# Layer 1 attention: the weights of each unit's last chunk are summed by TensorE instead of GpSimd

## The chip, the core and the metric

The kernel runs as one program on one core of a Trainium2 chip. Its engines are TensorE (PE, with PEld for its weight loads), VectorE (DVE), ScalarE (ACT), GpSimd (POOL) and SyncE (SP), which issues the transfers; each has its own queue and runs it in order, and they meet at semaphores. The metric is the time of one execution on the device in microseconds, the median of several. A profiled execution has a time of its own, and the lines shown come from one such execution.

## The reference

Two layers of attention over a picture of 2 batches, 256 channels and 64 x 64 places (4096 positions). The first layer has four heads of 16, a layer norm, a gate and a sigmoid; the change does not touch it. The second layer is

```python
qkv = einsum('oc,bchw->bohw', w_qkv, x) + b_qkv
q, k, v = split(qkv.reshape(b, 4, 3 * 64, 4096), 3, axis=2)
attn = softmax(einsum('bhdn,bhdm->bhnm', q, k) / 8, axis=-1)
out = einsum('bhnm,bhdm->bhnd', attn, v).reshape(b, 256, 64, 64)
return einsum('oc,bchw->bohw', w_out, out) + b_out + x
```

The softmax divides by the sum over all 4096 keys of the exponentials. It is these sums whose making is changed. All values are 32-bit floats.

## The kernel before, in words

**Units, chunks, steps.** Layer 1 works through 32 units: a batch, a pair of heads, and one of eight blocks of 512 queries. A unit goes over its 4096 keys in 32 chunks of 128, numbered 0 to 31. A chunk is a tile of 128 keys x (2 heads x 512 queries). Two chunks make a step, so a unit has 16 steps. The order of all work is written out by hand: the loop over steps at the end of the layer (L1219) calls the functions for the two chunks, here named first and second, at fixed places, and `at(step, place, ...)` hangs other work into the places "start", "early", "early end", "late" and "late end". Every engine keeps this order.

**What a step does.** `score` (L850) makes the scores of both chunks on PE into a tile of PSUM each; there are two such tiles, so the next scores wait until ACT has copied these out. `keep` (L867): DVE takes the running maximum (L878) over the chunk, then ACT copies the scores (L879) into a ring of 24 tiles called raw. Ten steps later, when the maximum over half of the chunks (16) is known, `shift` (L942) lets DVE subtract it in place (L944), `weigh` (L951) lets ACT take the exponential in place (L956), and `gather` (L970) lets PE multiply the weights with the values (av, L978). The maximum of a half reaches DVE through `turn_max`, `fold`, `split`, `turn` and `spread_shift`: PE turns it, DVE and POOL finish it, and a last product (L939) spreads it over the partitions. For the first half of a unit that product stands in step 10 of the unit itself. So a unit is weighed ten to eleven steps behind its scores, and its last two chunks (30 and 31) are gathered in step 10 of the next unit.

**The sums.** In `weigh`, after the exponential, POOL adds the chunk into an accumulator of its half (L966 for the first two chunks of a half, L968 for the others), so 30 adds a unit. In step 12 of the next unit `total` (L998) lets PE sum each accumulator over its 128 partitions by a product with ones (L1008, four products) into a tile called sum1, which `keep_total` (L1013) lets ACT copy out. The result then is turned and inverted, and scales the rows of the output (L1049). Near the end of the last unit, from chunk number `LATE` on, some chunks are not added by POOL: `on_tensor` (L948) picks them, and `gather` lets PE sum them directly by products of the weights with ones (L988) into a tile late_sums. Chunk 31 of the last unit is one of them.

**The bank that others share.** `misc` (L787) is a pool of a single PSUM tile. Keys and values of a later head pair (k1p, v1p: steps 4 to 7, in the first 24 units), queries (q1p, steps 14 and 15), the turned maxima (rt, nm1p: steps 0, 1, 8, 9), sum1 (step 12), the turned sums and outputs (steps 13 and 14) and the output projections take it in turn; the next user's first product waits until the last reader of the user before is done.

**The output projections.** The eight output blocks of batch 0 are projected while units 18 to 21 run, two in each: `fetch_output` (L1099) loads the block, `project_out` (L1081) lets PE make a half of the channels (L1083, in two products), `output` (L1089) lets DVE add bias and input (L1091) and stores the block after the second half. A block's first half is hung into step 3 or 11 of a unit, its second half into step 7 or 15.

Of the kernel before, what the change touches and what calls it, by code (L numbers as in the profile page):

```python
# [8 lines left out]
F32 = mybir.dt.float32  # L9
# [6 lines left out]
P = 128  # L16
NB = 512
# [10 lines left out]
def conv_attention_kernel(  # L28
# [20 lines left out]
    B, _, N = x.shape  # L49
    NJ = N // NB  # L50
    NM = N // P
# [75 lines left out]
    for s in range(3):  # L127
        t = const_prep.tile([P, CC, P], F32, tag=f"wpad{s}", name=f"wpad{s}")
# [27 lines left out]
    for i in range(2):  # L156
        t = const0.tile([P, PB, P], F32, tag=f"negmax0_{i}", name=f"negmax0_{i}")
# [66 lines left out]
    def at(t, place, step):  # L224
        extras.setdefault((t, place), []).append(step)
# [19 lines left out]
    with own0:  # L245
# [322 lines left out]
        for n, u in enumerate(units0):  # L568
# [6 lines left out]
            if u == units0[-1]:  # L575
                t1 = t0 + NM + 9
# [5 lines left out]
            else:  # L582
                t1 = t0 + NM + 15
# [79 lines left out]
        def misc(name):  # L663
            return small_bank[0](name)

        def fetch(key, src, tag="xb", bufs=3, pool=l1x):
            t = pool.tile([P, CC, NB], F32, tag=tag, bufs=bufs, name=f"{tag}_{key}")
            nc.sync.dma_start(out=t, in_=src.rearrange("(c p) n -> p c n", p=P))
            loaded[key] = t
# [52 lines left out]
        for i in range(NJ):  # L722
            k = (0, 0, i)
            t1 = T0 + 2 + 2 * i
# [3 lines left out]
            t1 = T0 + 20 + 3 * i if i < PB else END0 + (2, 3, 4, 9)[i - PB]  # L728
# [45 lines left out]
    END = len(units) * US  # L774


    LATE = len(units) * NM - 2 * LAG
    with (
        tc.tile_pool(name="l1", bufs=2) as l1,
# [9 lines left out]
        avs1, srows, losts, joined, halves = {}, {}, {}, {}, {}  # L789
# [13 lines left out]
        first, begun = {}, set()  # L803
# [37 lines left out]
        def next_queries(u, c):  # L841
            b, g, j = u
            if c == 0:
                q = l1x.tile([P, NB], F32, tag="q", name=f"q1_{b}_{g}_{j}")
                qs1[u] = q, misc(f"q1p_{b}_{g}_{j}")
            project_in(qs1[u][1], loaded["q", u], g, 0, c)
            if c == CC - 1:
                loaded.pop(("q", u))
# [99 lines left out]
        def on_tensor(t):  # L948
            return t >= LATE and (t % 2 == 1 or t < LATE + 4)

        def weigh(t):  # L951
            u = b, g, j = units[t // NM]
            m = t % NM
            n = m // GS
            p = raws[t]
            seq(nc.scalar.activation(p, p, AF.Exp, scale=D1**-0.5))  # L956

            if on_tensor(t):
                return
            if (u, n) not in first:  # L960
                first[u, n] = p
            elif (u, n) not in accs:
                accs[u, n] = l1.tile(
                    [P, 2, NB], F32, tag="acc", bufs=3, name=f"acc_{b}_{g}_{j}_{n}"
                )
                seq(nc.gpsimd.tensor_tensor(accs[u, n], first[u, n], p, ALU.add))  # L966
            else:
                seq(nc.gpsimd.tensor_tensor(accs[u, n], accs[u, n], p, ALU.add))  # L968

        def gather(t):  # L970
            u = b, g, j = units[t // NM]
            m = t % NM
            n = m // GS
            if m % GS == 0:
                avs1[u, n] = psv.tile([P, NB], F32, tag="av", name=f"av1_{b}_{g}_{j}_{n}")
            v = vs[b, g, m // PB]
            for k in range(2):
                seq(nc.tensor.matmul(  # L978
                    avs1[u, n][k * D1 : (k + 1) * D1, :], v[:, m % PB, k, :], raws[t][:, k, :],
                    start=(m % GS == 0), stop=(m % GS == GS - 1),  # L980
                ))
            raws.pop(t - 1, None)
            if on_tensor(t):
                if u not in srows:
                    srows[u] = psp.tile([P, 2, NB], F32, tag="pair", name="late_sums")[:, 0, :]
                for k in range(2):
                    r = D1 * n + 32 * k
                    seq(nc.tensor.matmul(  # L988
                        srows[u][r : r + 32, :], ones[:, :32], raws[t][:, k, :],
                        start=r not in begun, stop=False, skip_group_check=True,  # L990
                    ))
                    begun.add(r)
            if m % GS == GS - 1:
                a = l1.tile([P, NB], F32, tag="avs", name=f"avs1_{b}_{g}_{j}_{n}")
                seq(nc.scalar.copy(a, avs1.pop((u, n))))
                avs1[u, n] = a

        def total(u):  # L998


            b, g, j = u
            late = u in srows
            if not late:
                srows[u] = misc(f"sum1_{b}_{g}_{j}")
            for n in range(NG):
                for k in range(2):
                    r = D1 * n + 32 * k
                    seq(nc.tensor.matmul(  # L1008
                        srows[u][r : r + 32, :], ones[:, :32], accs[u, n][:, k, :],
                        start=not late, stop=True, skip_group_check=late,  # L1010
                    ))

        def keep_total(u):  # L1013
# [75 lines left out]
        def output(b, j, o):  # L1089
            xt = loaded["xo", b, j]  # L1090
            seq(nc.vector.scalar_tensor_tensor(  # L1091
                xt[:, o, :], outs.pop((b, j, o)), bo1[:, o : o + 1], xt[:, o, :], ALU.add, ALU.add
            ))
            if o == CC - 1:
                nc.sync.dma_start(
                    out=out[b, :, bass.ts(j, NB)].rearrange("(c p) n -> p c n", p=P), in_=xt
                )
# [11 lines left out]
        for n, u in enumerate(units):  # L1109
            b, g, j = u  # L1110
            t0 = n * US
            if n > 0:
                at(t0 - 5, "start", lambda u=u, b=b, j=j: fetch(("q", u), x1[b][j]))
                at(t0 - 2, "late", lambda u=u: next_queries(u, 0))
                at(t0 - 1, "early", lambda u=u: next_queries(u, 1))
                at(t0 - 1, "early end", lambda u=u: keep_queries(u))
            if n < len(units) - NJ:
                to = (*units[n + NJ][:2], j)
                at(t0 + 1, "start", lambda to=to: fetch(("kv", *to), x1[to[0]][to[2]]))
                for c in range(CC):  # L1120
                    at(t0 + 4 + c, "early", lambda to=to, c=c: next_keys(*to, c))
                at(t0 + 5, "early end", lambda to=to: store_keys(*to))
                at(t0 + 6, "early", lambda to=to: next_values(*to, 0))
                at(t0 + 7, "early", lambda to=to: next_values(*to, 2))
                at(t0 + 7, "early end", lambda to=to: store_values(*to))

                t1 = (n // NJ * NJ + NJ - 1) * US
                at(t1 + 2 * j + 2, "start", lambda to=to: load_keys(*to))
                at(t1 + 2 * j + 3 + LAG, "start", lambda to=to: load_values(*to))
            for k in range(NG):  # L1130
                t1 = t0 + (k + 1) * GS // 2
                at(t1, "early", lambda u=u, k=k: turn_max(u, k, 0))
                at(t1, "early end", lambda u=u, k=k: fold(u, k, 0))
                at(t1, "late", lambda u=u, k=k: turn_max(u, k, 1))
                at(t1, "late end", lambda u=u, k=k: (fold(u, k, 1), split(u, k)))
                at(t1 + 1, "late", lambda u=u, k=k: turn(u, k))
                at(t1 + 2, "early", lambda u=u, k=k: spread_shift(u, k))
            t1 = t0 + US + GS // 2
            at(t1 + 4, "early", lambda u=u: total(u))
            at(t1 + 4, "early end", lambda u=u: keep_total(u))  # L1140
            at(t1 + 5, "early", lambda u=u: turn_total(u))
            at(t1 + 5, "early end", lambda u=u: factors(u))
            at(t1 + 5, "late", lambda u=u: turn_sums(u, 1))
            at(t1 + 5, "late end", lambda u=u: rows(u, 1))
            at(t1 + 6, "early", lambda u=u: turn_sums(u, 0))
            at(t1 + 6, "early end", lambda u=u: rows(u, 0))
            if b < B - 1 and (g, j) == (PR - 1, NJ - 1):
                for i in range(NJ):
                    t1 = t0 + US + (i + 4) * GS // 2
                    at(t1, "start", lambda b=b, i=i: fetch_output(b, i))  # L1150
                    for o in range(CC):
                        at(
                            t1 + 3 + 4 * o, ("early", "late")[o],
                            lambda b=b, i=i, o=o: project_out(b, i, o, misc(f"o1_{b}_{i}_{o}")),
                        )
                        at(t1 + 3 + 4 * o, "late end", lambda b=b, i=i, o=o: output(b, i, o))

# [59 lines left out]
        for t in range(max(t for t, _ in extras) + 1):  # L1219
            inside, behind = 0 <= t < END, 0 <= t - LAG < END  # L1220
            pair = (2 * t, 2 * t + 1)
# [83 lines left out]
```

## Time and profile before

| | |
|---|---|
| time, median of 3 runs (lowest to highest) | 4742.49 us (4742.18 to 4742.6) |
| the profiled execution: its time, its span | 4741.58 us, 4739.8 us |
| granted TensorE clock, mean | 0.996 |
| layer 1, from the first running maximum (2062.95) to 4695: PE, DVE, POOL, ACT busy | 2460, 2455, 2385, 2187 of 2632 us |
| a unit, from its first running maximum to the next unit's (2124.79 to 2206.09) | 81.30 us |
| a unit with two output blocks (3596.50 to 3685.25) | 88.75 us |
| a unit of the last eight, without keys and values for others (4262.34 to 4341.52) | 79.18 us |
| POOL adds: L968 x884, L966 x64 | 2.373 us and 2.381 us each |

How to read it: a line of a timeline has the start in us, the time from first start to last end, the engine, the line of the kernel, the operation, output <- inputs, the shapes and how often; in brackets the idle time of the engine just before it, and which engine and line ended that. The releaser is inferred from semaphore events. Matmuls are pipelined and their ends are modelled, so the distance between starts tells more about PE than an end does. A 32-bit product has two rows in the profile ("x2") for each product in the code. Busy shares of a whole execution mix the layers; the tables by window give them for one unit.

### The profile page before, as it was taken

The page shows a single profiled execution, that of the slowest core. Times are in us where ns is not written, and L with a number is a line of the kernel's source. Part 1 is how long each engine was busy: PE and PEld are TensorE (multiplying, and loading weights), DVE is VectorE, ACT ScalarE, POOL GpSimd, SP SyncE. Part 2 cuts the span into 40 slices and gives each one's busy share as a digit, 9 for nine tenths or more (in the row PEclk, how much of TensorE's full clock was granted, in tenths as well). Part 3 has the DMA queues.
Part 4 walks back from the last instruction along what each step waited for, and adds up shares of the span by engine and source line. Part 5 has one row for each costly group of instructions (what it writes and reads, how often), then busy time and mean ns, then how long its engine had stood idle before and what let it go on. Part 6 is the DMA issues. An engine that isn't in the chain of part 4 may idle for free.

```text
span 4739.8 us, 70643 instructions
## 1 busy us (share of the span) xinstructions
PE 4526.9 (96%) x27506; PEld 1496.2 (32%) x27506; DVE 3917.0 (83%) x4584; ACT 3394.1 (72%) x4508; POOL 2540.6 (54%) x1491
## 2 busy tenths in 40 slices
PE   8999999999999999989999999999999999999998
PEld 3433333333333333333232232323233332222222
DVE  6777777777777777359999999999999899999996
ACT  3366666666666666668888888888887778888884
POOL 6300000000000000039999999999998889999994
PEclk9999999999999999999999999999999999999999
DMA  3100000000000000110000100001111111000002
GB/s 103 34 4 19 19 21 15 15 15 15 15 15 15 15 13 13 57 63 25 23 25 17 54 30 23 25 23 36 52 36 45 63 52 47 18 14 7 14 16 74
DMA packets 113381, 140.10 MB, mean 30 GB/s; under 512 B 51864, under 2 KB 52696, under 8 KB 112932
## 3 DMA queue, kind: packets, MB, share of 16 engines
q1 hardware_dynamic: 111260, 135.11, 9.2%
q8 instruction: 216, 3.54, 0.3%
q14 instruction: 121, 0.99, 0.1%
q10 hardware_dynamic: 1784, 0.46, 0.0%
HBM read 93.58 MB, written 41.70 MB: 29 GB/s over the span
## 4 chain that ended last, share of the span: by engine, by line
PE 58%; DVE 15%; POOL 15%; issue 6%; ACT 5%; DMA 1%; SPq 0%; ACTq 0%; DVEq 0%; POOLq 0%
PE s L448 24%; POOL acc L968 13%; PE av L463 12%; DVE rmax L878 10%; PE s L861 6%; PE av L978 5%; DVE raw L944 4%; ACT raw L879 4%; PE a L410 2%; PE p L270 1%; PE k1p L672 1%; POOL acc L966 1%; PE rt L886 1%; PE q1p L672 1%; PE o L549 1%
## 5 line engine op out<-in xcount | busy, mean ns | idle before, releaser
L968 POOL TENSOR_TENSOR acc<-acc,raw 128x1024 f32<-128x1024 f32 x884 | 2098.1, 2373 | 89.4 <-ACT raw L956 30.2
L414 DVE TENSOR_REDUCE mx<-a 128x1 f32<-128x512 f32 x2048 | 1315.3, 686 | 450.5 <-PE a L410 449.4
L451 ACT ACTIVATE p<-s 128x512 f32<-128x512 f32 x2048 | 1109.8, 597 | 701.3 <-PE a L410 367.3
L944 DVE TENSOR_TENSOR raw<-raw,shift 128x1024 f32<-128x1024 f32 x1024 | 1238.0, 1213 | 19.2 <-PE shift L939 12.7
L861 PE MATMUL s<-q,k 64*128 64x512 f32 x4096 | 1117.2, 636 | 142.9 <-ACT raw L879 134.6
L878 DVE TENSOR_TENSOR rmax<-s,rmax 128x1024 f32<-128x1024 f32 x960 | 1170.1, 1219 | 72.7 <-PE s L861 70.8
L879 ACT COPY raw<-s 128x1024 f32<-128x1024 f32 x1024 | 1037.7, 1013 | 259.4 <-DVE rmax L878 173.5
L448 PE MATMUL s<-q,kT 32*128 32x512 f32 x4096 | 1219.1, 640 | 0.0
L956 ACT ACTIVATE raw<-raw 128x1024 f32<-128x1024 f32 x1024 | 1086.9, 1062 | 178.4 <-DVE raw L944 147.3
L410 PE MATMUL a<-kT,q 32*128 32x512 f32 x4096 | 1129.7, 643 | 1.2 <-DVE mx L414 1.0
L978 PE MATMUL av<-raw,v 128*64 128x512 f32 x4096 | 999.3, 606 | 2.0
L463 PE MATMUL av<-p,v 128*32 128x256 f32 (+1 forms) x7904 | 650.2, 399 | 0.6 <-ACT avs L477 0.6
L861 PEld LDWEIGHTS s<-q,k 64*128 64x128 f32 x4096 | 317.1, 185 | 827.9 <-ACT raw L879 628.0
L513 POOL TENSOR_TENSOR f<-f,dyn 128x16 f32<-128x16 f32 x15 | 3.3, 223 | 1028.2 <-DVE f L512 1028.2
L448 PEld LDWEIGHTS s<-q,kT 32*128 32x128 f32 x4096 | 397.9, 183 | 426.3 <-issue 392.1
L978 PEld LDWEIGHTS av<-raw,v 128*64 128x64 f32 x4096 | 243.3, 136 | 587.6 <-issue 428.8
L463 PEld LDWEIGHTS av<-p,v 128*32 128x32 f32 x7904 | 157.6, 108 | 751.5 <-issue 737.3
L564 POOL TENSOR_SCALAR res<-res 128x1024 f32<-128x1024 f32 x16 | 16.8, 1049 | 660.5 <-ACT res L563 660.5
L410 PEld LDWEIGHTS a<-kT,q 32*128 32x128 f32 x4096 | 305.0, 184 | 31.4 <-DVE mx L414 18.2
L966 POOL TENSOR_TENSOR acc<-raw,raw 128x1024 f32<-128x1024 f32 x64 | 152.4, 2381 | 112.7 <-ACT raw L956 103.8
L898 DVE TENSOR_REDUCE negs<-rt 128x4 f32<-128x512 f32 x128 | 88.3, 690 | 50.1 <-PE rt L886 47.6
L318 DVE RECIPROCAL std<-std 128x128 f32<-128x128 f32 x64 | 56.1, 920 | 37.7 <-ACT std L313 37.7
(332 smaller groups left out, 1840.4 us busy)
## 6 DMA issues: line engine op xcount, KB each, us to landing
x<-in_x_dram SPq DMA_DIRECT2D x16, 512.0 KB
res<-in_x_dram SPq DMA_DIRECT2D x16, 512.0 KB
x<-res SPq DMA_DIRECT2D x16, 512.0 KB
att<-rows SPq DMA_DIRECT2D x62, 128.0 KB
kd<-k1s SPq DMA_DIRECT2D x24, 256.0 KB
vd<-v1s SPq DMA_DIRECT2D x24, 256.0 KB
k<-kd SPq DMA_DIRECT2D x24, 256.0 KB
v<-vd SPq DMA_DIRECT2D x24, 256.0 KB
```

The lines of the kernel that those rows point to most:

```text
L410: seq(nc.tensor.matmul(ps, qs0[u][r, bass.ts(i, P)], kTs[b][r, bass.ts(m, NB)], start=True, stop=True,))
L414: seq(nc.vector.tensor_reduce(mxs[u][:, i * H + h, m : m + 1], ps, AX.X, ALU.max))
L448: seq(nc.tensor.matmul(ps, kTs[b][r, bass.ts(m, P)], qs0[u][r, :], start=True, stop=True))
L451: seq(nc.scalar.activation(pt[:, k, :], ps, AF.Exp, scale=D0**-0.5))
L463: seq(nc.tensor.matmul(avs[u][32 * h : 32 * h + 32, cols], vs0[b][:, m, 32 * h : 32 * h + 32], pts[t, h // 2][:, h % 2, cols], start=(m == ...
L861: seq(nc.tensor.matmul(ps[:, k, :], ks[b, g, m // PB][r, bass.ts(m % PB, P)], qs1[u][r, :], start=True, stop=True,))
L878: seq(nc.vector.tensor_tensor(rmax[u, n], ps, before, ALU.max))
L879: seq(nc.scalar.copy(raw, ps))
L944: seq(nc.vector.tensor_tensor(raws[t], raws[t], shifts[u, t % NM // GS], ALU.add))
L956: seq(nc.scalar.activation(p, p, AF.Exp, scale=D1**-0.5))
L968: seq(nc.gpsimd.tensor_tensor(accs[u, n], accs[u, n], p, ALU.add))
L978: seq(nc.tensor.matmul(avs1[u, n][k * D1 : (k + 1) * D1, :], v[:, m % PB, k, :], raws[t][:, k, :], start=(m % GS == 0), stop=(m % GS == GS ...
```

## The change

Chunk 31 of every unit is treated like the chunks that `on_tensor` picks: POOL does not add it, and PE sums it in `gather`, right behind the av products of the chunk, by two products with ones (for the two heads), into the tile that `total` later adds the accumulators to. For all units but the last this tile is the misc bank, which the unit now takes in step 10 instead of step 12. The products of `total` for the second half go on from what is there. `begun` now remembers the unit too.

As the misc bank is taken in steps 10 to 12, the first halves of the projections that were hung into step 11 go to step 10; those of step 3 stay there. In both cases DVE's add for the first half moves from the end of the step ("late end") to its middle ("early end"), between the two chunks' running maxima.

```diff
@@ weigh
-            if on_tensor(t):
+            if on_tensor(t) or m == NM - 1:
                 return
@@ gather
-            if on_tensor(t):
+            if on_tensor(t) or m == NM - 1:
                 if u not in srows:
-                    srows[u] = psp.tile([P, 2, NB], F32, tag="pair", name="late_sums")[:, 0, :]
+                    if t >= LATE:
+                        srows[u] = psp.tile([P, 2, NB], F32, tag="pair", name="late_sums")[:, 0, :]
+                    else:
+                        srows[u] = misc(f"sum1_{b}_{g}_{j}")
                 for k in range(2):
                     r = D1 * n + 32 * k
                     seq(nc.tensor.matmul(
                         srows[u][r : r + 32, :], ones[:, :32], raws[t][:, k, :],
-                        start=r not in begun, stop=False, skip_group_check=True,
+                        start=(u, r) not in begun, stop=False, skip_group_check=True,
                     ))
-                    begun.add(r)
+                    begun.add((u, r))
@@ total
-            b, g, j = u
-            late = u in srows
-            if not late:
-                srows[u] = misc(f"sum1_{b}_{g}_{j}")
             for n in range(NG):
                 for k in range(2):
                     r = D1 * n + 32 * k
                     seq(nc.tensor.matmul(
                         srows[u][r : r + 32, :], ones[:, :32], accs[u, n][:, k, :],
-                        start=not late, stop=True, skip_group_check=late,
+                        start=(u, r) not in begun, stop=True, skip_group_check=True,
                     ))
@@ the output projections of batch 0, t1 = the step at which block i is fetched
                     for o in range(CC):
+                        step = t1 + (3 - i % 2, 7)[o]
                         at(
-                            t1 + 3 + 4 * o, ("early", "late")[o],
+                            step, ("early", "late")[o],
                             lambda b=b, i=i, o=o: project_out(b, i, o, misc(f"o1_{b}_{i}_{o}")),
                         )
-                        at(t1 + 3 + 4 * o, "late end", lambda b=b, i=i, o=o: output(b, i, o))
+                        at(
+                            step, ("early end", "late end")[o],
+                            lambda b=b, i=i, o=o: output(b, i, o),
+                        )
```

## The prediction

> **What bounds the kernel now.** I read the page first: shares of busy time, the chain that ended last, the group of the moved operation.
>
> ```profile
> PE 4526.9 (96%) x27506; PEld 1496.2 (32%) x27506; DVE 3917.0 (83%) x4584; ACT 3394.1 (72%) x4508; POOL 2540.6 (54%) x1491
> PE 58%; DVE 15%; POOL 15%; issue 6%; ACT 5%; DMA 1%; SPq 0%; ACTq 0%; DVEq 0%; POOLq 0%
> L968 POOL TENSOR_TENSOR acc<-acc,raw 128x1024 f32<-128x1024 f32 x884 | 2098.1, 2373 | 89.4 <-ACT raw L956 30.2
> ```
>
> POOL, whose adds the change shortens, holds 15% of the chain. That has to be tested in one unit, since shares mix two layers. Next the table of busy times over three units, each window running from one unit's first running maximum to the next's (columns: window and length, then busy time of PE, PEld, DVE, ACT, POOL, clock, DMA share, GB/s):
>
> ```profile
> 3019.09:3100.54 81.45, 76.84 (x330) 24.34 (x328) 76.36 (x74) 68.40 (x74) 75.69 (x43) 1.00 0.07 23
> 3596.50:3685.25 88.75, 83.64 (x346) 27.41 (x344) 79.07 (x76) 68.69 (x74) 75.40 (x43) 1.00 0.17 57
> 4262.34:4341.52 79.18, 72.83 (x310) 21.64 (x308) 76.06 (x73) 67.87 (x72) 75.41 (x43) 1.00 0.04 11
> ```
>
> PE, DVE and POOL are each 93 to 94% busy in the first. DVE and POOL have nearly the same work in the third, which lacks the keys and values of another head pair (k1p, v1p: about 4.2 us of PE) and is 2.1 us shorter with the usual period of 81.3. In the second, four output projections (7.7 us of PE) make it 7.45 us longer. So PE time lengthens a unit while POOL's is the same in all three. Last, the order of time around step 10 of a unit, where the new matmuls go: PE, then DVE, then POOL.
>
> ```profile
> 3068.49 0.38 PE L939 MATMUL shift<-mrow,ones 64*128 64x512 bf16 x2
> 3068.80 1.94 PE L978 MATMUL av<-raw,v 128*64 128x512 f32 x8
> 3070.67 1.13 PE L861 MATMUL s<-q,k 64*128 64x512 f32 x4
> 3072.51 1.13 PE L861 MATMUL s<-q,k 64*128 64x512 f32 x4 [0.72 <-ACT raw L879]
> 3080.94 2.21 PE L861 MATMUL s<-q,k 64*128 64x512 f32 x8
> ```
> ```profile
> 3068.98 1.22 DVE L944 TENSOR_TENSOR raw<-raw,shift 128x1024 f32<-128x1024 f32 x1 [0.34 <-POOL acc L968]
> 3070.12 1.22 DVE L878 TENSOR_TENSOR rmax<-s,rmax 128x1024 f32<-128x1024 f32 x1
> 3072.38 1.22 DVE L878 TENSOR_TENSOR rmax<-s,rmax 128x1024 f32<-128x1024 f32 x1
> 3082.11 1.23 DVE L878 TENSOR_TENSOR rmax<-s,rmax 128x1024 f32<-128x1024 f32 x1 [0.60 <-PE s L861]
> ```
> ```profile
> 3064.15 7.30 POOL L968 TENSOR_TENSOR acc<-acc,raw 128x1024 f32<-128x1024 f32 x3
> 3073.99 2.38 POOL L966 TENSOR_TENSOR acc<-raw,raw 128x1024 f32<-128x1024 f32 x1 [2.54 <-ACT raw L956]
> ```
>
> A bound DVE maximum starts 1.17 us after its score matmuls (3080.94 to 3082.11). The next pair of scores after step 10 starts at 3070.67 and could be used at 3071.84; DVE comes to it at 3072.38. So PE is 0.54 us early here: that is all the slack an insertion has. The three adds of the POOL line are of chunks 29, 30, 31; the third ends at about 3071.4, its reader (the sum at L1008) starts at 3078.07, and POOL idles 2.54 us right behind it.
>
> **The change part by part.**
>
> *POOL loses 31 adds of 2.373 us (73.6 us): taken at nothing.* The removed add is the one ahead of POOL's idle time, which ACT's exponential ends, so nothing after it on POOL starts earlier; POOL's idle time becomes some 4.9 us. The ring slot that it also freed is next written by ACT's copy at 3075.95, 4.5 us later. POOL's name in the chain rests on the label at 3068.98. In the unit with projections the same DVE instruction (3649.54, idle 0.35) starts 0.49 us after the same shift matmul (3649.05) and is put down to PE; 3068.49 to 3068.98 is 0.49 too. The add that ends at that moment is of chunk 30 and stays. Bounds: nothing, or at most the labelled 0.34 plus the 0.16 that ACT's copy at 3071.45 is said to wait for POOL.
>
> *PE gains 62 matmuls, 124 rows, one group of four rows per unit, in 31 units (the last had them).* The late sums of the last unit are the same operation: groups at 4676.85 and 4679.70 with the av matmuls at 4677.83 between them, so 0.98 us each. The weight loads (108 ns) are inside. They stand behind av and ahead of both scores of step 11, in PE's order. 0.98 less the 0.54 of slack delays that DVE maximum by 0.44 us. Queued behind it on DVE: shift, second maximum. From there the delay goes on: maximum to ACT copy 1.31 (3074.64 to 3075.95), copy to the next scores 1.07 (3077.02), then sum, av, scores and the wait at 3082.11, all later by 0.44; DVE's 0.60 there cannot swallow it, being fed from DVE. Cross-check by other insertions: k1p and v1p are four groups of 1.06 to 1.09 us, and cost 2.11 us a unit (81.30 less 79.19), so 0.53 each and 0.55 swallowed each. Bounds: 0 (swallowed later) and 0.98 (no slack). I take 0.44, the value that both rows give: 27 units without projections x 0.44 = 11.9 us. The new sums tile holds the single misc bank from step 10 to 12; before it, nm1p is copied away by 3067.96, and no other user comes between, but for the projections.
>
> *The projections in the four units 18 to 21.* In step 3 the DVE add (L1091) moves ahead of the second maximum. PE's projection ends at 3611.9, so the add waits until 3612.01 and the maximum moves from 3611.05 to 3612.67 (+1.62). But DVE idled 0.88 us before the next maximum (3614.94), and the moved add gives 0.66 back: that one keeps its time. ACT's copy ends at 3614.99, so the next scores start at 3615.04 for 3614.74: +0.3. Bounds 0 and 1.62. For the other block the projection moves from step 11 to 10, where the program's order puts it ahead of the shift matmul: 1.92 us of PE at 3649.05, so DVE's shift goes from 3649.54 to 3651.46, and with the add (0.66) the second maximum is 2.57 late. Step 11 loses both: its next maximum (3659.09, after 0.88 idle) comes at 3660.04, +0.95; along copy, scores, sum, av the one at 3663.87 is 1.27 late, and the rows product at 3668.28, which idled 0.46, 0.85. I take 1.0 (between the two last), with the four new rows included: they run beside the moved add. Bounds 0 and 2.57. The second projection of each block (2.5 us of DVE idle at 3635.94) stays. No DMA is added; the attention block issued at 3635.93 has its packets in by 3641, 8 us before its earlier use. Sum: 4 x (0.3 + 1.0) = 5.2 us.
>
> *Sum:* 11.9 + 5.2 = 17.1 us. The profiled execution took 4741.58 (span 4739.8), 0.9 below the median of the runs, 4742.49. 4742.49 + 17.1 = 4759.6.
>
> A rule weighed against the rows: 0.98 us of PE busy time in a unit where PE is 94% busy. The Trainium skill, Perfetto Trace Analysis, section Identifying the Most-Contended Engine, says that matmul busy time misleads and that weight-load busy share tells TensorE's headroom; that is 24.3 of 81.5 us here, 30%, and by it the new matmuls would be free (4747.7). The rows of k1p and v1p decide against it: PE's order, not its capacity, delays DVE.
>
> **The rivals.**
> - *POOL is on the path after all.* For it: 15% of the chain. The labelled waits of 0.34 and 0.16 go with the add: 31 x 0.50 = 15.5 us gained; with the projections 4742.5 - 15.5 + 5.2 = 4732, and faster. It decides only if the adds ahead of 3068.98 end earlier, by more than the 0.44 that PE adds; they stand before the removed one.
> - *Swallowed.* A later PE or DVE wait absorbs the 0.44; the projections alone remain: 4742.5 + 5.2 = 4747.7, no measurable change. Against: k1p and v1p are not absorbed.
> - *No slack.* The matmuls cost 0.98 in all 31 units, for instance because scores start later behind matmuls that are 32 columns wide: 30.4 + 5.2, so 4778. Against: the same 0.54 stands in every unit looked at.
>
> **How the numbers follow.** Forecast 0.80, POOL 0.05, swallowed 0.09, no slack 0.06. The forecast's own range: 0.30 to 0.58 a unit in 31 units (9 to 18) and projections 0 to 10, so 4752 to 4769. To hold 8 in 10 with room for the swallowed case: 4747 to 4770. A measurement of this kernel tells about 0.2% (9.5 us) from no change. Faster by more: 0.05, the POOL case. Within: 0.10, the swallowed case and the forecast's low edge. Slower: 0.85.
>
> **What would show it.** Usual period 81.3 becomes 81.7, the last units' 79.2 becomes 79.6, the projecting units' 88.75 becomes about 90; a DVE wait of about 0.44 for PE appears at the first maximum of step 11; POOL idles about 4.9 us once a unit; DVE's 0.34 at the first shift stays. Wrong if the period stays or falls, if a sums row takes far from 0.98 a group, or if the units of the projections shrink.

## The result: 0.39% slower, and the profile after

The changed kernel takes 4760.63 us (median of 6 runs, 4759.13 to 4762.22); the kernel before, run beside it, 4742.30 us (4741.69 to 4742.60). The ratio is 1.0039, 95% interval 1.0029 to 1.0049. The forecast was 4759.6.

The page after (busy shares, the chain that ended last, the group of POOL's adds):

```profile
PE 4553.5 (96%) x27630; PEld 1502.2 (32%) x27630; DVE 3919.4 (82%) x4584; ACT 3393.9 (71%) x4508; POOL 2464.6 (52%) x1460
PE 66%; DVE 18%; issue 8%; ACT 5%; POOL 2%; DMA 1%; SPq 0%; ACTq 0%; DVEq 0%; POOLq 0%
L969 POOL TENSOR_TENSOR acc<-acc,raw 128x1024 f32<-128x1024 f32 x853 | 2023.1, 2372 | 82.9 <-ACT raw L957 26.1
```

PE has 124 more rows, POOL 31 adds fewer, 75 to 76 us less of busy time. POOL's share of the chain falls from 15% to 2%, and the kernel is slower. A reader who goes by the share alone sees an engine taken off the critical path here.

The table of busy times over three units, each window from one unit's first running maximum to the next's (window and length; busy PE, PEld, DVE, ACT, POOL; clock; DMA share; GB/s): a usual unit, a projecting one, one of the last eight.

```profile
3106.03:3187.76 81.73, 77.35 (x334) 24.51 (x332) 76.42 (x73) 68.57 (x74) 72.97 (x41) 1.00 0.08 23
3605.73:3696.01 90.28, 85.32 (x351) 27.47 (x348) 79.05 (x77) 68.66 (x74) 72.94 (x42) 1.00 0.18 55
4278.34:4357.98 79.64, 73.58 (x314) 21.80 (x312) 76.17 (x74) 67.94 (x72) 73.00 (x41) 1.00 0.04 11
```

The lengths were 81.30 (usual), 88.75 and 79.18: up by 0.44 (81.74 in most of the usual units), 1.53 and 0.45. POOL is busy 2.4 to 2.7 us less in each, which shortens none. From the first unit's first maximum to the last unit's it is 2534.47 us for 2516.35, 18.1 more, and that is 27 x 0.445 + 4 x 1.53: the whole difference lies in these periods.

The timelines of PE, DVE and POOL around steps 10 and 11 of a usual unit:

```profile
3155.72 1.94 PE L979 MATMUL av<-raw,v 128*64 128x512 f32 x8
3157.59 1.05 PE L992 MATMUL sum<-raw,ones 128*32 128x512 f32 x4
3158.57 1.99 PE L862 MATMUL s<-q,k 64*128 64x512 f32 x8
```
```profile
3155.90 1.22 DVE L945 TENSOR_TENSOR raw<-raw,shift 128x1024 f32<-128x1024 f32 x1 [0.34 <-POOL acc L969]
3158.17 1.21 DVE L945 TENSOR_TENSOR raw<-raw,shift 128x1024 f32<-128x1024 f32 x1
3159.75 1.23 DVE L879 TENSOR_TENSOR rmax<-s,rmax 128x1024 f32<-128x1024 f32 x1 [0.36 <-PE s L862]
3169.49 1.22 DVE L879 TENSOR_TENSOR rmax<-s,rmax 128x1024 f32<-128x1024 f32 x1 [0.60 <-PE s L862]
```
```profile
3151.07 4.81 POOL L969 TENSOR_TENSOR acc<-acc,raw 128x1024 f32<-128x1024 f32 x2
3160.90 2.37 POOL L967 TENSOR_TENSOR acc<-raw,raw 128x1024 f32<-128x1024 f32 x1 [5.02 <-ACT raw L957]
```

DVE's shift ahead of the same maximum (3072.38) in the kernel before:

```profile
3071.25 1.21 DVE L944 TENSOR_TENSOR raw<-raw,shift 128x1024 f32<-128x1024 f32 x1
```

The new products hold PE from 3157.59 to the scores at 3158.57, 0.98 us. DVE then waits for those scores, where it had not waited: its maximum starts 1.58 us after the shift ahead of it instead of the usual 1.13, so 0.45 late (the 0.36 in brackets is less because two DVE instructions overlap by 0.09 in the profile when they run back to back). The wait of 0.60 further on is as before, so nothing of it is given back. POOL idles 5.02 us in place of 2.54. DVE's 0.34 "for POOL" is still there; the add that it names is that of chunk 30, which POOL keeps.

### The profile page after: what moved, and what is told of

The parts are those of the page before. It is cut to its first block, busy times and chain, and to the rows that moved or that the text cites. A ratio compares the mean times of both kernels' runs of the same rounds, so it can differ in the third digit from the quotient of the medians.

```text
span 4757.3 us, 70829 instructions
## 1 busy us (share of the span) xinstructions
PE 4553.5 (96%) x27630; PEld 1502.2 (32%) x27630; DVE 3919.4 (82%) x4584; ACT 3393.9 (71%) x4508; POOL 2464.6 (52%) x1460
## 4 chain that ended last, share of the span: by engine, by line
PE 66%; DVE 18%; issue 8%; ACT 5%; POOL 2%; DMA 1%; SPq 0%; ACTq 0%; DVEq 0%; POOLq 0%
PE s L448 24%; PE av L463 12%; DVE rmax L879 12%; PE s L862 9%; PE av L979 8%; DVE raw L945 5%; ACT raw L880 5%; PE a L410 2%; POOL acc L969 2%; PE p L270 1%; PE rt L887 1%; PE k1p L672 1%; PE v1p L705 1%; PE q1p L672 1%; PE o L549 1%
## 5 line engine op out<-in xcount | busy, mean ns | idle before, releaser
L969 POOL TENSOR_TENSOR acc<-acc,raw 128x1024 f32<-128x1024 f32 x853 | 2023.1, 2372 | 82.9 <-ACT raw L957 26.1
```

## The experiments

Each kernel is compared with the kernel before, run on the same chip beside it (medians 4741.07 to 4742.34). "Units" gives the period of a usual unit, a projecting one, and one of the last eight.

### Is POOL on the path? The kernel before without the 31 adds

```diff
@@ weigh, in the kernel before
-            if on_tensor(t):
+            if on_tensor(t) or m == NM - 1:
                 return
```

> The kernel before, with POOL's add of chunk 31 of every unit left out and nothing put in its place: that chunk is missing from the sum of every unit but the last. My theory (POOL is not on the path): no change, 4742.3 us, the unit stays at 81.30 us, and POOL idles about 4.9 us ahead of the next L966 for 2.54. Rival (POOL is on the path, as its share of the chain says): 31 x 0.50 = 15.5 us gained, 4727 us, and the waits put down to POOL at the first shift (0.34) and at ACT's copy (0.16) are gone.

Measured: 4741.24 us for 4741.93, ratio 0.9999 (0.9989 to 1.0008); units 81.28, 88.73, 79.18. The shares of the chain, the timelines of DVE and POOL around step 10, and DVE's in the same step of a later unit:

```profile
PE 63%; DVE 16%; POOL 8%; issue 6%; ACT 6%; DMA 1%; ACTq 0%; DVEq 0%; POOLq 0%
```
```profile
3069.44 1.22 DVE L944 TENSOR_TENSOR raw<-raw,shift 128x1024 f32<-128x1024 f32 x1 [0.34 <-POOL acc L968]
```
```profile
3074.44 2.38 POOL L966 TENSOR_TENSOR acc<-raw,raw 128x1024 f32<-128x1024 f32 x1 [5.02 <-ACT raw L956]
```
```profile
3232.13 1.22 DVE L944 TENSOR_TENSOR raw<-raw,shift 128x1024 f32<-128x1024 f32 x1 [0.35 <-PE shift L939]
```

ACT's copy, which had waited "for POOL" where the removed add ended, in the kernel before and then in this run:

```profile
3071.45 1.01 ACT L879 COPY raw<-s 128x1024 f32<-128x1024 f32 x1 [0.16 <-POOL acc L968]
```
```profile
3071.91 1.01 ACT L879 COPY raw<-s 128x1024 f32<-128x1024 f32 x1 [0.15 <-DVE rmax L878]
```

The work taken off POOL is all turned into idle time. Both waits in POOL's name are labels. ACT's names the removed add; without that add it is as long as before and put down to DVE. DVE's names the add of chunk 30, which is still made, so its staying proves nothing by itself. But DVE starts 0.49 us after the shift matmul in every unit from the second on, in the kernel before and here; at 3232.13 POOL's add ends only 0.15 us after DVE has started, and there the same wait is put down to PE. In this kernel's chain POOL has 8%, in that of the kernel before 15%, at the same time: the share changes by what happens to end last at each step, not by what can be gained.

### How does the cost depend on the size? Half the products, half the columns, twice the products

```diff
@@ gather, the new products: the first head's alone
-                for k in range(2):
+                for k in range(2 if on_tensor(t) else 1):
@@ or: over half of the queries
+                    w = NB if on_tensor(t) else NB // 2
...
-                        srows[u][r : r + 32, :], ones[:, :32], raws[t][:, k, :],
+                        srows[u][r : r + 32, :w], ones[:, :32], raws[t][:, k, :w],
@@ and total, which then writes over them
-                        start=(u, r) not in begun, stop=True, skip_group_check=True,
+                        start=u != units[-1], stop=True, skip_group_check=True,
@@ or: both made twice
-                for k in range(2):
+                for k in ((0, 1) if on_tensor(t) else (0, 1, 0, 1)):
```

> The changed kernel with one of the two new products per unit: chunk 31 is missing from the sum of the second head of each pair, in every unit but the last. My theory (0.54 us of slack at that place): 0.49 us of PE fits into the slack, so the usual unit is back at 81.30 us and the last ones at 79.2; only the four units with projections stay 1.53 us longer than before: 4742.3 + 6.1 = 4748.4 us. Rival (PE time costs in proportion, wherever it stands): 0.22 us a unit, 81.52, and 4742.3 + 6.1 + 27 x 0.22 = 4754.3 us.

Measured: 4759.63 us for 4741.93, ratio 1.0036 (1.0023 to 1.0050); units 81.73, 90.27, 79.62. Both expectations missed. PE's timeline tells why:

```profile
3155.79 1.05 PE L992 MATMUL sum<-raw,ones 128*32 128x512 f32 x2
3156.77 1.57 PE L862 MATMUL s<-q,k 64*128 64x512 f32 x6
```

One product (two rows) holds PE for 0.98 us, as long as the two did. So the run did not halve the inserted time; it repeated the changed kernel. The two products write to different groups of 32 output partitions (64 to 95 and 96 to 127), and run beside each other: in the changed kernel's trace their rows start 0.01 us apart. The Trainium skill, TensorE: Matmul & The Clock Gate, Part 3: Packing small matmuls, says that such products run at the same time in separate column groups; this pair of runs agrees, 0.98 us for one and 0.98 for two. That the rule bore on the halved kernel was overlooked in its expectation. Halving the columns does halve the time:

> The changed kernel with the new products of chunk 31 over half of the 512 queries, and the rest of the sum then written over them: chunk 31 is left out of the sums of all units but the last. The products then hold PE for about 0.5 us in place of 0.98, which the 0.54 us of slack covers. Theory (slack first, then delay): usual units 81.30, last units 79.2, projecting units 90.2 at most, total 4747 to 4749. Rival (the delay is in proportion to the time on PE): usual units 81.5, total 4742.3 + 27 x 0.22 + 5.5 = 4754.

Measured: 4749.01 us for 4742.34, ratio 1.0013 (1.0004 to 1.0023); units 81.32, 90.23, 79.22. PE's timeline:

```profile
3153.04 0.63 PE L993 MATMUL sum<-raw,ones 128*32 128x256 f32 x4
3153.60 1.13 PE L862 MATMUL s<-q,k 64*128 64x512 f32 x4
```

Inserted 0.56 us; the usual unit grows by 0.02.

> The changed kernel with the two new products of each unit made twice, so chunk 31 counts twice in the sums. My theory (cost = time inserted less 0.54): 1.96 - 0.54 = 1.42 us a unit, the usual unit 82.72 us, the last ones 80.6; in the units with projections about 1.06 more than now, 91.3: 4742.3 + 27 x 1.42 + 4 x 2.6 = 4791 us. Rival (PE time costs in proportion, 0.45 of it): 0.88 us a unit, 82.18, and 4742.3 + 27 x 0.88 + 4 x 2 = 4774 us.

Measured: 4786.33 us for 4741.93, ratio 1.0094 (1.0077 to 1.0111); units 82.59, 91.12, 80.49. PE's timeline:

```profile
3167.18 1.91 PE L992 MATMUL sum<-raw,ones 128*32 128x512 f32 x8
3169.02 1.56 PE L862 MATMUL s<-q,k 64*128 64x512 f32 x6
```

Inserted 1.84 us (not the 1.96 expected), the usual unit grows by 1.29. So three sizes lie on one line, inserted time less 0.54:

| inserted ahead of the scores, us | less 0.54 | growth of a usual unit, us |
|---|---|---|
| 0.56 (half the columns) | 0.02 | 0.02 |
| 0.98 (the change) | 0.44 | 0.44 |
| 1.84 (twice) | 1.30 | 1.29 |

### Does the place decide? The new products between the two scores of step 11

The same products, issued one score later: behind the first of the two scores of step 11 instead of ahead of both.

```diff
@@ gather: the products of chunk 31 are put off (sum_chunk makes them, as in the change)
-            if on_tensor(t) or m == NM - 1:
...
+            if on_tensor(t):
+                sum_chunk(t, raws[t])
+            elif m == NM - 1:
+                waiting.append(lambda t=t, raw=raws[t]: sum_chunk(t, raw))
@@ the loop over the steps
-            scores = [score(c) for c in pair] if inside else []
+            scores = []
+            for c in pair if inside else ():
+                scores.append(score(c))
+                while waiting:
+                    waiting.pop()()
```

> The changed kernel with the two new products moved behind the first scores of step 11, where PE waits 0.72 us for ACT in the kernel before; same work, same result. My theory (the place decides, not the amount): the second scores of step 11 start 0.12 us later and have 0.96 us of slack, so the usual unit is 81.30 us again and only the moved projections remain: between 4742.3 + 5.2 = 4747.5 and 4742.3 + 6.1 = 4748.4 us. Rival (PE's total time is what costs): 81.74 us a unit and 4760 us, as the changed kernel.

Measured: 4747.43 us for 4741.93, ratio 1.0012 (1.0003 to 1.0021); units 81.28, 90.22, 79.17. PE's timeline:

```profile
3151.40 1.13 PE L862 MATMUL s<-q,k 64*128 64x512 f32 x4
3152.46 1.05 PE L983 MATMUL sum<-raw,ones 128*32 128x512 f32 x4
3153.44 1.13 PE L862 MATMUL s<-q,k 64*128 64x512 f32 x4
```

The second score waited 0.72 us for ACT at this point; the products now fill that time, DVE has no wait behind them, and the usual unit is as long as before the change. PE is busy as much as in the changed kernel (4557.7 us for 4553.5). What is left, 5.5 us, stands in the projecting units.

### What do the two parts cost by themselves?

The projections' steps alone (the second part of the diff, applied to the kernel before), and the sums alone (the first part; the projections stay, and units 17 to 20, whose chunk 31 would meet a projection in the bank, keep POOL's add):

```diff
@@ weigh and gather of the changed kernel, for the sums alone
-            if on_tensor(t) or m == NM - 1:
+            if on_tensor(t) or (m == NM - 1 and t // NM not in range(17, 21)):
```

> The kernel before with only the projections' new steps (no product for chunk 31, POOL keeps its 31 adds). Theory (the projections' steps cost by themselves, about 1.5 us in each of four units, as the changed kernel's 90.28 for 88.75 shows): usual units 81.30, projecting units 90.2, last units 79.2, total 4742.3 + 4 x 1.5 = 4748. By the prediction's own terms (1.3 a unit) 4747.5. Rival (the 1.5 us comes from the new products beside them, in the shared bank): projecting units 88.8 to 89.2, total 4742 to 4744.

Measured: 4747.87 us for 4742.34, ratio 1.0012 (1.0003 to 1.0021); units 81.30, 90.23, 79.18.

> The changed kernel with the projections at their old steps; the four units whose chunk 31 would meet a projection in the bank keep POOL's add. So the new products stand in 27 units, with no projection beside them. Theory: usual units 81.74, last units 79.63, projecting units 88.75 as before, total 4742.3 + 27 x 0.44 = 4754.2. Together with the kernel that has the projections' steps alone it makes up the whole 18.3 us. Rival (parts act on each other): the two together miss the whole by more than 2 us.

Measured: 4754.19 us for 4742.34, ratio 1.0026 (1.0016 to 1.0035); units 81.75, 88.74, 79.64. The parts come to 5.5 and 11.9 us, 17.4 together, against 18.3 for both: the parts hardly act on each other.

The run with the projections alone shows where its 1.48 us per unit arise. Set beside the unit of the kernel before, from the same first maximum, DVE's maxima are on time up to step 4 (but for the one behind the moved add of step 3, 1.61 late, made good at once), 0.44 late from step 5 on (0.32 in step 6), 3.12 late behind the moved projection of step 10, 1.49 late in step 12, 1.92 in step 13, and 1.48 from step 14 to the end of the unit. PE's timelines around step 4, of the kernel before and then of this run, whose unit starts 0.84 later:

```profile
3613.76 1.99 PE L861 MATMUL s<-q,k 64*128 64x512 f32 x8
3615.68 1.12 PE L672 MATMUL k1p<-xb_('kv', 1, 1, 3)_28401,w 128*128 128x512 f32 x2
```
```profile
3614.60 1.13 PE L861 MATMUL s<-q,k 64*128 64x512 f32 x4
3615.90 1.13 PE L861 MATMUL s<-q,k 64*128 64x512 f32 x4 [0.17 <-ACT raw L879]
3616.95 1.13 PE L672 MATMUL k1p<-xb_('kv', 1, 1, 3)_28401,w 128*128 128x512 f32 x2
```

The second score starts at 3615.90, which is 3615.06 in the time of before; the prediction had 3615.04. But the next matmul starts 1.05 us behind it, where the unbroken group of eight rows takes 1.92 for both scores, 0.96 each. So k1p starts 0.43 late and not 0.3: 0.34 for the later start (3614.72 before) and 0.09 for the longer score.

### Can the place be used? Keys and values between the scores

If the place decides, the four insertions of keys and values for another head pair (k1p and v1p), which cost 2.11 us a unit, should cost less between scores. All the following start from the kernel before, with POOL's adds.

```diff
@@ the loop over the steps
-            scores = [score(c) for c in pair] if inside else []
+            scores = [score(pair[0])] if inside else []
+            hung(t, "between")
+            if inside:
+                scores.append(score(pair[1]))
@@ keys and values of unit n
-                at(t0 + 1, "start", lambda to=to: fetch(("kv", *to), x1[to[0]][to[2]]))
+                steps = (4, 5, 6, 7) if n in range(18, 22) else (3, 4, 6, 7)
+                place = "early" if n in range(18, 22) else "between"
+                at(max(t0 - 2, 0), "start", lambda to=to: fetch(("kv", *to), x1[to[0]][to[2]]))
                 for c in range(CC):
-                    at(t0 + 4 + c, "early", lambda to=to, c=c: next_keys(*to, c))
-                at(t0 + 5, "early end", lambda to=to: store_keys(*to))
-                at(t0 + 6, "early", lambda to=to: next_values(*to, 0))
-                at(t0 + 7, "early", lambda to=to: next_values(*to, 2))
-                at(t0 + 7, "early end", lambda to=to: store_values(*to))
+                    at(t0 + steps[c], place, lambda to=to, c=c: next_keys(*to, c))
+                at(t0 + steps[1], "early end", lambda to=to: store_keys(*to))
+                at(t0 + steps[2], place, lambda to=to: next_values(*to, 0))
+                at(t0 + steps[3], place, lambda to=to: next_values(*to, 2))
+                at(t0 + steps[3], "early end", lambda to=to: store_values(*to))
```

This is the second of four such kernels; the first had steps 3, 4, 10 and 11.

> The kernel before (POOL keeps its adds, projections stay) with the four insertions of keys and values of the next head pair (1.06 to 1.09 us each) moved from behind the scores of steps 4 to 7 to between the two scores of steps 3, 4, 10 and 11, where the second score waits 0.45 to 0.94 us for ACT anyway; in the four projecting units they stay. Theory (the place decides, not the amount of PE work): 1.0 to 2.1 us less in each of 20 units, so usual units 79.2 to 80.3 and total 4742.3 - 20 to 42, thus 4700 to 4722. Rival (PE's whole work of a unit sets its time): usual units stay at 81.3, total 4742.

Measured: 4748.31 us for 4742.34, ratio 1.0013 (1.0004 to 1.0023); units 81.51, 88.75, 79.18. A miss. The timelines of PE and DVE in step 10:

```profile
3070.28 1.16 PE L705 MATMUL v1p<-w,xb_('kv', 1, 0, 4)_24871 128*128 128x128 f32 x8 [0.89 <-ACT mrow L930]
```
```profile
3072.82 1.22 DVE L944 TENSOR_TENSOR raw<-raw,shift 128x1024 f32<-128x1024 f32 x1 [1.92 <-PE shift L939]
```

The misc bank still holds nm1p there, until ACT has copied it; the values wait 0.89 us for that, and DVE 1.92 us for the shift matmul queued behind them. It is the wait, not the idea, that ate the gain: steps 6 and 7, where the bank is free, were tried next.

> As the run with the keys and values between scores, but the values at steps 6 and 7 (the keys stay at 3 and 4), where the small PSUM bank is free; in that run the values at step 10 waited 0.89 us for ACT's copy of the row in the bank, and DVE 1.92 us behind the shift matmul after them. In the projecting units all four stay as in the kernel before. Theory (place decides, and that run lost its gain to the bank alone): the keys' 0.42 us of DVE wait remains, the values add 0 to 0.5, so usual units 79.6 to 80.2 for 81.30, total 4742.3 - 20 x (1.1 to 1.7), thus 4708 to 4720. Rival (PE's whole work of a unit sets its time): usual units 81.3, total 4742.

Measured: 4719.79 us for 4741.07, ratio 0.9954 (0.9939 to 0.9969); units 80.06, 88.75, 79.18. PE's timeline in step 7 and DVE's behind it:

```profile
3038.09 1.13 PE L861 MATMUL s<-q,k 64*128 64x512 f32 x4
3039.15 1.16 PE L705 MATMUL v1p<-w,xb_('kv', 1, 0, 4)_24871 128*128 128x128 f32 x8
3040.24 1.13 PE L861 MATMUL s<-q,k 64*128 64x512 f32 x4
```
```profile
3044.34 1.23 DVE L878 TENSOR_TENSOR rmax<-s,rmax 128x1024 f32<-128x1024 f32 x1 [0.46 <-PE s L861]
```

The same work costs 0.87 us a unit instead of 2.11. Each pair of insertions ends in one DVE wait of 0.43 or 0.46, so the cover is not complete. The input of these products is also fetched three steps earlier than before, but that is not the gain: in the kernel before PE was never idle ahead of one of them. The first unit is 63.93 us long for 61.84, of which up to 1.1 may be scatter, since the kernels that leave this unit as it was have 61.7 to 63.0. Its load is issued no earlier than step 0 while its use moved forward; whether that is the cause was not looked into.

Two more, with the keys at steps 3 and 5 and step 12's sum products between scores as well, and then the projecting units treated the same way:

```diff
@@ keys at steps 3 and 5, and the sum products of step 12
-                steps = (4, 5, 6, 7) if n in range(18, 22) else (3, 4, 6, 7)
+                steps = (4, 5, 6, 7) if n in range(18, 22) else (3, 5, 6, 7)
-            at(t1 + 4, "early", lambda u=u: total(u))
+            at(t1 + 4, "between", lambda u=u: total(u))
@@ in the last one also
-                place = "early" if n in range(18, 22) else "between"
+                place = "between"
-                            t1 + 3 + 4 * o, ("early", "late")[o],
+                            t1 + 3 + 4 * o, ("between", "late")[o],
-                        at(t1 + 3 + 4 * o, "late end", lambda b=b, i=i, o=o: output(b, i, o))
+                        at(t1 + 3 + 4 * o, ("early end", "late end")[o], lambda b=b, i=i, o=o: output(b, i, o))
```

> As the one before it, with the keys at steps 3 and 5 instead of 3 and 4, and the eight sum products of step 12 moved between that step's two scores too (in all 31 units). Theory (each insertion of about 1 us between scores is covered when 0.45 to 0.65 us of waiting and 0.54 of slack are there each time): usual units 78.6 to 79.4, last units 78.6 to 79.0, total 4742.3 - 20 x (1.9 to 2.7) - 8 x 0.4, thus 4685 to 4702. Rival (PE's whole work sets the time): 81.3 and 4742.

Measured: 4722.68 us for 4741.07, ratio 0.9961 (0.9947 to 0.9975); units 80.19, 88.74, 79.18. A miss: moving the sum products took DVE's wait of 0.60 behind step 12 away, but DVE's timeline has it again a little later, in front of the rows:

```profile
3073.90 0.69 DVE L1049 TENSOR_TENSOR rows<-turned,f 128x512 f32<-128x512 f32 x1 [0.67 <-PE turned L1023]
```

In the unit shown that wait had been 0.16; in most others it is 0.54 where there was none. The last eight units, which only this move touches, stay at 79.18, so the 0.13 us by which a usual unit is longer than in the run before is put down to the keys at steps 3 and 5, which were not tried alone.

> As the one before it, and in the four projecting units too the keys and values (steps 4 to 7) and the first projection of each block (steps 3 and 11, its DVE add right behind the first shift) between the scores. Theory: projecting units 85 to 87.5 for 88.75, so 5 to 15 us less in total than the run before it. Rival (a projection of 1.92 us is too long for a wait of 0.5 to 0.9 and DVE stalls behind it): projecting units 88.75 or more, total as the run before it.

Measured: 4716.56 us for 4741.07, ratio 0.9948 (0.9933 to 0.9962); units 80.18, 87.40, 79.17. This is the fastest of all, 44 us faster than the changed kernel, and it computes all that the kernel before does, with POOL's adds kept.

## Why the prediction was right

- **POOL's adds at nothing: shown.** The prediction read POOL's idle time behind the removed add as room that stays empty; leaving out the adds alone moved the time by 0.01%, with 0.1% to either side. That the 0.34 is a label, and its real end the shift matmul, is borne out by the 0.49 us from that matmul in every unit, however POOL's add lies; and the 0.16 stayed when the add that it names was gone.
- **0.98 less 0.54, 0.44 a unit: shown.** Its three parts were measured apart: 0.98 in the PE line, 0.54 as the point from which the cost starts (0.56 costs 0.02), and no part of the 0.44 given back (DVE's 0.60 unchanged). The rival "swallowed" falls with the changed kernel's units, "no slack" with the same 0.44 and with the run over half of the columns. That the reason is the order on PE and not its load is shown by the same products one score later, at no cost.
- **The projections: mechanism right, size short.** The prediction had 0.3 for step 3 and 1.0 for steps 10 and 11, 5.2 us in four units. Measured 0.44 and 1.04, and 0.05 for the new rows beside them: 1.53, so 6.1 us. The mis-sized term is step 3's 0.3: the start of the second score was right to 0.02 us, but a score that starts after a wait was taken to last as long as one inside a group of eight, 0.96, and it takes 1.05. In the other block the steps on the way were 0.1 to 0.2 off (the second maximum 2.68 late for 2.57, the next 1.05 for 0.95, the one after 1.48 for 1.27, each without step 3's 0.44), and the value taken, 1.0, was near the 1.04 that reached the end. As it was a choice between 0.85 and 1.27, and the steps under it were off, that nearness is in part luck. Together 18.1 us where 17.1 were predicted, and this 1 us is all that the forecast missed. One slip in its range: 18 and 10 on top of 4742.5 make 4770.5 and not 4769, and the 18 is reckoned for 31 units where the sum has 27.
- **The rule weighed in the prediction: this case decides against taking it as a price.** By weight-load time PE had 70% to spare (24.5 of 81.73 us after), and yet 0.98 us more on PE cost 0.44 a unit at one place and nothing at another. The Trainium skill, Perfetto Trace Analysis, section Identifying the Most-Contended Engine, gives a measure of PE's distance from its peak. That an insertion is free by it was the prediction's own step, and it fails; what an insertion costs here is read from the wait of the instruction behind it.

Of what was to be seen, all was: 81.7, 79.6, about 90 (90.28), the DVE wait (0.45 late, printed as 0.36), POOL idle (5.02 for 4.9), the label at 0.34.

## What to carry to other kernels

Price an insertion into an in-order queue at the place where it stands: its own time less the slack of the first instruction behind it that another engine waits for; on this kernel the same 0.98 us cost 0.44 or nothing, one instruction apart. Where an engine waits for a buffer at a regular place, move work into that wait, but first ask who holds the buffers that the moved work needs. Before giving an engine's work away because it has a large share of the chain, leave that work out once: if the time stays, the share was a label.

## What was not expected of the hardware

- A product with 32 output rows costs as much PE time alone as two that write to different groups of 32 output partitions: 0.98 us for one and for two. Four products in two groups take 1.84.
- A score group of four rows holds PE for 1.05 to 1.06 us when a wait or other work stands beside it, and 0.96 inside a group of eight (1.92). So splitting a pair of scores costs about 0.2 us of PE's time (2 x 1.06 less 1.92), 0.1 for each score. This was read from several lines, not tried by a run of its own.
